# Zeros by GpSimd and twelve idle products at the start of a relative-attention and binary-FFN kernel

## The chip, the cores and the metric

The kernel runs on one core of a Trainium2 chip. The metric is the device time of one execution in microseconds (us), as the median of several runs. The core has five engines with a queue each: TensorE (PE), which multiplies matrices, VectorE (DVE), ScalarE (ACT), GpSimd (POOL) and SyncE (SP), which here only issues transfers. Engines wait for one another through semaphores.

## The reference

The input x has 16 blocks (the batch) of 512 rows with 128 features. Each row is normalised, and the result xn goes two ways. Both results are added to x.

```python
xn = _layernorm(x)
# attention: 16 heads of 8, with relative positions
xa = layernorm(xn) * ln_g + ln_b
q, k, v = xa @ Wq + bq, xa @ Wk + bk, xa @ Wv + bv
p = pe @ Wp                                    # pe: sines and cosines of the position
score = (q + u_bias) k^T + relative_shift((q + v_bias) p^T)
attn = softmax(score * 8 ** -0.5) v
out_a = attn @ Wo + bo
# FFN with weights of +1 and -1 from boolean kernels k0, k1, k2
h = relu(s0 * [xn, -xn] @ k0) * 2
h = relu(s1 * h @ k1) * 2
out = x + out_a + s2 * h @ k2
```

## The kernel before

The program has two stages. The first, up to about 240 us, normalises the blocks, runs the FFN and the projections, and writes q + u, q + v, k, p and v to DRAM in the layout that the second stage reads. The second, from there to the end, is the attention, head by head, in an order written out by hand (`STEPS`), with a few last pieces of the FFN beside its first steps.

In the first stage no order is written by hand on any engine, but for a few single edges (`issue_after`). The program is traced in the order of the source, and a planner of the framework then sets the order on each engine: of the instructions that it reckons to be ready, by its own costs of the operations and transfers, it takes the one that stands earliest in the source. The engines run their queues strictly in the order that results. An instruction that the planner reckoned ready too early so holds up all that stands behind it on its engine.

What bears on the change, in the order of the source:

- L266 to L270: `root` and `rows` are filled by VectorE, and ScalarE takes a first square root.
- L280: `qu_t` are the two tiles for the halves of q + u: `k_flat[0]`, a tile of the second stage, and `qu_l`, each of 128 x 2050 float16, zeroed as 1025 words. q + u is written to every second place in part of them, and the zeros beside it are written out with it. `after` (L274) are two places in the buffer `e_1`, in which p lies between zeros for a while. `v_t` (two tiles) are filled with ones. `q_banks` (L236) are two PSUM banks for q.
- L288 to L293: these fills. VectorE fills `qu_t` and `after`, GpSimd fills `v_t`.
- L294 to L323: SyncE issues the loads, one after the other: block 0 of x, k0, the three scales `s_cols`, k1, block 1 of x, k2, the weights, and so on.
- L325 to L330: GpSimd makes the identity `ident` and tables from it.
- L339 to L386, `norm(0)`: VectorE takes the statistics of block 0 (L365, L366), ScalarE the root (L375), VectorE the reciprocal and one refinement step (L376 to L382), then normalises the four chunks (L351). `norm(1)` and later ones are called from a queue further down, and take the statistics of blocks 1 and 2, 3 and 4 and so on.
- L395 to L407: from `s_cols` and k0 VectorE makes the factors `w_mul` and the first FFN weights (L402); ScalarE makes the second weights from k1 (L404), four instructions.
- L441 and L449: the tile `ab` of 128 x 2 x 128 float32 is filled with ones by GpSimd. One half of it is later scaled (L461), and both are the stationary operands of three products (L467 to L475), which bound the sizes of q and k.
- L530 to L541, `transposed2`: TensorE transposes the four chunks of a block (L534), ScalarE and VectorE split the result into a high and a low float16 half (L624, L625). The low half is what the high one leaves of the value.
- L659 to L662, `ffn_layer`: for each f of four, TensorE multiplies the weights with the high and then the low half (L644), and ScalarE and VectorE split the result (L621, L622).
- L485 to L499: the scales of q, k and p come out of VectorE (L487 scales Wp), and L499 is the first product of the projections.
- L664 and L694: `ffn_residual` loads x again for the sum at the end of a block, `ffn_out` adds to it (L700) and stores it (L703).

Of the kernel before, what the change touches and what calls it, by code (L numbers as in the profile page):

```python
# [9 lines left out]
F32 = mybir.dt.float32  # L10
# [9 lines left out]
B, S, D, H, DH = 16, 512, 128, 16, 8  # L20
P = 128
# [67 lines left out]
def rel_attention_and_binary_ffn(  # L89
# [38 lines left out]
    nc = tc.nc  # L128
# [102 lines left out]
    with ExitStack() as pre:  # L231
# [4 lines left out]
        q_banks = psp.tile([P, 2, S], F32, tag="q", name="q_banks")  # L236
# [8 lines left out]
        def sts(name, shape, dt=F32):  # L245
            return setup.tile(shape, dt, tag=name, name=name)
# [38 lines left out]
        qu_rows = [t[:, : 4 * S].rearrange("p (v x) -> p v x", v=2) for t in qu_t]  # L285
        v_b = [t.rearrange("p (h c w) -> p h c w", h=H, c=NC) for t in v_t]

        for t in qu_t:  # L288
            nc.vector.memset(t.bitcast(F32), 0.0)
        for t in after:  # L290
            nc.vector.memset(t.rearrange("p x u b -> p (x u b)").bitcast(F32)[:, : PAD + S // 2], 0.0)
        for t in v_t:
# [145 lines left out]
                nc.vector.tensor_copy(cols, pt[:, :10])  # L438


        ab = sts("ab", [P, 2, D])  # L441
        t_abs = sts("t_abs", [P, 3])
        w_abs = sts("w_abs", [P, 3, D])
        rows_abs = sts("rows_abs", [4, 2, P])
# [1 line left out]
        pw = sts("pw", [P, 2])  # L446
        q_mul, k_mul = pw[:, 0:1], pw[:, 1:2]
        b_cols = sts("b_cols", [P, 3])
        nc.gpsimd.memset(ab, 1.0)  # L449

        def absolute():
            for dst, src in (
# [758 lines left out]
```

## Time and profile before

| | |
|---|---|
| median of 3 runs | 1342.36 us |
| lowest, highest run | 1341.71, 1346.67 us |
| profiled execution | 1341.79 us |
| its span, first to last instruction | 1339.8 us |
| mean granted clock of TensorE | 0.994 |
| first record of TensorE | 9.86 us |
| first product of the FFN | 12.29 us |
| end of GpSimd's first fills and the identity | 2.55 us |

The profile is of one execution. Its times run from the first instruction; the execution takes 2.0 us more than its span. A group of instructions is named by its line in the source. "Busy" is the share of time in which an engine runs an instruction; records of TensorE overlap, so that for a row of products the distance from start to start says more than the length of one. A float32 product stands as two records. "The chain" is followed back from the last instruction, at each step to what released it.

### The profile page before, as it was taken

What the parts mean: (1) busy time and instruction counts of PE and PEld (TensorE: products, weight loads), DVE (VectorE), ACT (ScalarE), POOL (GpSimd) and SP (SyncE); (2) the same over time, 40 slices, a digit from 0 to 9 for tenths busy, and PEclk for the clock granted to TensorE, in tenths of its full rate; (3) what the DMA queues carried; (4) which work ended last, traced back from release to release, by engine and by line L of the source; (5) the groups of instructions that cost most, each with busy time, mean ns of one, the idle gap of its engine ahead of it and who ended that gap; (6) DMA issues with size and microseconds to landing.
All of it is one profiled execution on the core that took longest, in us unless ns stands there. A gap on an engine that the chain in (4) does not pass through costs nothing.

```text
span 1339.8 us, 55726 instructions
## 1 busy us (share of the span) xinstructions
PE 1290.1 (96%) x23065; PEld 948.2 (71%) x23065; DVE 1117.1 (83%) x2734; ACT 851.2 (64%) x1389; POOL 305.8 (23%) x520
## 2 busy tenths in 40 slices
PE   6899999889999999999999999999999999999995
PEld 3455555677777777777777777777777777777763
DVE  8999766778888888888888888888888888888874
ACT  4555666556666666666666666666666666666660
POOL 3011000112222222222233322222222222233100
PEclk9999999999999999999999999999999999999998
DMA  5576548944444444444444444444444445544443
GB/s 143 200 252 214 209 176 309 304 108 108 111 109 105 105 105 107 107 105 106 109 110 112 106 110 113 107 119 116 119 116 123 110 116 134 119 106 115 102 94 79
DMA packets 278409, 178.07 MB, mean 133 GB/s; under 512 B 113142, under 2 KB 266780, under 8 KB 278084
## 3 DMA queue, kind: packets, MB, share of 16 engines
q1 hardware_dynamic: 258940, 157.10, 42.5%
q0 software_dynamic: 16880, 16.30, 5.3%
q8 instruction: 181, 2.97, 1.0%
q10 hardware_dynamic: 2336, 1.12, 0.3%
q14 instruction: 72, 0.59, 0.2%
HBM read 113.97 MB, written 56.78 MB: 127 GB/s over the span
## 4 chain that ended last, share of the span: by engine, by line
PE 82%; DVE 8%; DMA 5%; ACT 2%; issue 1%; SPq 1%; POOL 0%; POOLq 0%; DVEq 0%; ACTq 0%
PE a_t L908 18%; PE s L881 17%; PE s L819 17%; PE s L835 12%; PE p L644 6%; PE t_t L872 4%; PE s L848 4%; DMA q<-qv_scr 1%; DVE m L867 1%; PE a_t L686 1%; DVE h2l L622 1%; DVE qu_l L526 1%; DVE xn L351 1%; PE p L579 1%; DMA rden_scr<-den 1%
## 5 line engine op out<-in xcount | busy, mean ns | idle before, releaser
L891 ACT ACTIVATE e<-s,e_scale 128x512 f32<-128x512 f32 x1024 | 672.6, 685 | 334.7 <-PE s L881 334.4
L862 DVE TENSOR_REDUCE m<-s 128x256 bf16<-128x512 f32 x512 | 351.4, 686 | 127.5 <-PE s L848 127.4
L867 DVE TENSOR_TENSOR m<-s,m 128x256 bf16<-128x256 f32 x1024 | 429.6, 420 | 18.3 <-PE s L848 0.6
L819 PE MATMUL s<-q,k 128*128 128x64 f16 x8192 | 407.0, 193 | 2.4 <-DVE e L622 1.6
L881 PE MATMUL s<-ident_b,nm 128*128 128x256 bf16 x2048 | 352.6, 274 | 2.3 <-DVE nm L876 2.3
L835 PE MATMUL s<-q,win 128*128 128x128 f16 (+1 forms) x4096 | 342.5, 206 | 0.0
L819 PEld LDWEIGHTS <-k 128*128 128x128 f16 x8192 | 335.2, 98 | 9.3 <-issue 3.0
L908 PE MATMUL a_t<-e,v 128*9 128x256 f32 x4032 | 265.3, 380 | 0.7 <-issue 0.7
L835 PEld LDWEIGHTS <-win 128*128 128x128 f16 x4096 | 232.0, 98 | 0.0
L881 PEld LDWEIGHTS <-nm 128*128 128x128 bf16 x2048 | 144.8, 98 | 118.1 <-DVE m L867 78.0
L848 PE MATMUL s<-q,win_d 128*128 128x64 f16 x2048 | 227.7, 193 | 0.0
L876 DVE TENSOR_REDUCE nm<-t_t 128x2 bf16<-128x256 bf16 x512 | 209.3, 409 | 0.6 <-PE t_t L872 0.6
L872 PE MATMUL t_t<-ident_b,m 128*128 128x128 bf16 x1024 | 141.1, 219 | 5.4 <-DVE m L867 5.3
L966 POOL DMA_DIRECT2D rden_scr<-den x58 | 32.4, 559 | 489.9 <-DVE nm L876 465.5
L908 PEld LDWEIGHTS a_t<-e,v 128*9 128x9 f32 x4032 | 86.3, 90 | 80.9 <-issue 1.5
L848 PEld LDWEIGHTS <-win_d 128*128 128x128 f16 x2048 | 129.9, 98 | 0.0
L958 POOL DMA_DIRECT2D sum_scr<-av x232 | 117.5, 513 | 0.0
L872 PEld LDWEIGHTS <-m 128*128 128x128 bf16 x1024 | 79.6, 97 | 41.3 <-DVE m L867 10.7
L644 PEld LDWEIGHTS <-e 128*128 128x128 f16 x512 | 49.5, 98 | 59.5 <-issue 11.3
L644 PE MATMUL p<-h1l,e 128*128 128x512 f16 x240 | 63.2, 381 | 0.0
L644 PE MATMUL p<-h1h,e 128*128 128x512 f16 x240 | 62.2, 379 | 0.5 <-DVE h1l L622 0.5
L622 DVE SCALAR_TENSOR_TENSOR h2l<-p,h2h 128x512 f16<-128x512 f32 x60 | 41.1, 686 | 25.9 <-ACT h2h L621 25.7
(165 smaller groups left out, 894.7 us busy)
## 6 DMA issues: line engine op xcount, KB each, us to landing
q<-qv_scr SPq DMA_DIRECT2D x512, 64.0 KB
q<-qu_scr SPq DMA_DIRECT2D x256, 64.0 KB
k<-k_scr SPq DMA_DIRECT2D x128, 128.0 KB
win<-p_scr SPq DMA_DIRECT2D x128, 79.5 KB
v<-v_scr SPq DMA_DIRECT2D x32, 288.0 KB
k_scr<-hv SPq DMA_DIRECT2D x64, 128.0 KB
qu_scr<-k SPq DMA_DIRECT2D x16, 512.0 KB
qu_scr<-qu_l SPq DMA_DIRECT2D x16, 512.0 KB
```

Source lines behind the costliest of these rows:

```text
L644: nc.tensor.matmul(ph, lhsT=w[:, t, f * P : (f + 1) * P], rhs=h[t][m], start=(m == 0 and t == 0), stop=(m == 1 and t == n - 1),)
L819: nc.tensor.matmul(sp[:, c % 2, :, :, 4 * g : 4 * g + 4].rearrange("p a r (n m) -> p n (a r) m", m=2), lhsT=kt[:, g, c * P : (c + 1) * P], ...
L835: nc.tensor.matmul(blocks[:, x0 : x0 + (NC + 1) * (len(cs) - 1) + 1 : NC + 1], lhsT=win[side_m][:, side, y0 : y0 + P], rhs=qp[:, side, :, ...
L848: nc.tensor.matmul(blocks[:, x0 : x0 + NC + 2 : NC + 1, 2 * t : 2 * t + 2], lhsT=win_d[side_m][:, t, UP_OFF - 4 * u : WIND - 4 * u], rhs=q ...
L862: nc.vector.tensor_reduce(st["max"], flat(st["ps"][0]).rearrange("p c x -> p x c"), AX.X, ALU.max)
L867: nc.vector.tensor_tensor(st["max"], flat(st["ps"][1])[:, c], st["max"], ALU.max)
L872: nc.tensor.transpose(st["pt"][:, f, :], st["max"][:, f * P : (f + 1) * P], ident_b)
L876: nc.vector.tensor_reduce(st["nm"], st["pt"], AX.X, ALU.max, negate=True)
L881: nc.tensor.matmul(flat(st["ps"][half])[:, :, f * P : (f + 1) * P], lhsT=st["nm"][:, f : f + 1].to_broadcast([P, P]), rhs=ident_b.unsqueez ...
L891: nc.scalar.activation(st["eT"][:, :, cs, :, i0 : i0 + 4].rearrange("p b c a r -> p (c a) b r"), st["ps"][half].rearrange("p c a r b -> p ...
L908: nc.tensor.matmul(bank[32 * r : 32 * r + VW, g], lhsT=v_t[pair["m"]][:, v0 : v0 + VW], rhs=pair["eT"][:, b, c], start=(c == 0), stop=(c = ...
L958: queue.dma_start(sum_scr[h, :, b : b + 2, :], av[32 * r : 32 * r + DH])
```

## The change

Three edits, all at the start of the first stage. The tile `ab` is made, and filled with ones by GpSimd, ahead of all other fills. Right behind it in the source stand twelve float32 products of `ab` with itself, 128 x 128 times 128 x 256, into the two banks of q in turn; nobody reads the results. And the zeros in `qu_t` are written by GpSimd instead of VectorE; those in `after` stay with VectorE.

```diff
+        ab = sts("ab", [P, 2, D])
+        nc.gpsimd.memset(ab, 1.0)
+        for n in range(12):
+            nc.tensor.matmul(
+                q_banks[:, n % 2, : 2 * D],
+                lhsT=ab[:, 0],
+                rhs=ab.rearrange("p n d -> p (n d)"),
+                start=True,
+                stop=True,
+            )
+
         for t in qu_t:
-            nc.vector.memset(t.bitcast(F32), 0.0)
+            nc.gpsimd.memset(t.bitcast(F32), 0.0)
         for t in after:
             nc.vector.memset(t.rearrange("p x u b -> p (x u b)").bitcast(F32)[:, : PAD + S // 2], 0.0)
...
-        ab = sts("ab", [P, 2, D])
         t_abs = sts("t_abs", [P, 3])
...
-        nc.gpsimd.memset(ab, 1.0)
```

## The prediction

> **What bounds the kernel now.** I first asked where the whole span goes, then only about the stretch that the change touches. From the page, busy time and the chain of waits:
>
> ```profile
> span 1339.8 us, 55726 instructions
> ...
> PE 1290.1 (96%) x23065; PEld 948.2 (71%) x23065; DVE 1117.1 (83%) x2734; ACT 851.2 (64%) x1389; POOL 305.8 (23%) x520
> ...
> PE 82%; DVE 8%; DMA 5%; ACT 2%; issue 1%; SPq 1%; POOL 0%; POOLq 0%; DVEq 0%; ACTq 0%
> ```
>
> TensorE carries 82% of the chain and GpSimd none. All that the change edits happens before the first product of data, so the second view is the chain in its first 17 us: start, length, what.
>
> ```profile
> 3.25 4.13 DMA xn<-in_L_attn_x_dram
> ...
> 7.41 0.29 DVE bn L365
> 7.71 0.10 DVE root L376
> ...
> 8.11 2.93 ACT e L404 x4
> 11.04 0.52 ACT e L413
> 11.55 0.12 ACT w_abs L459
> 11.67 0.58 ACT sums L624
> 12.25 0.04 issue
> 12.29 1.45 PE p L644 x3
> 13.75 0.02 issue
> 13.77 0.61 ACT h1h L621
> 14.38 0.02 issue
> 14.40 0.69 DVE h1l L622
> ...
> 16.71 5.34 PE p L644 x24
> ```
>
> No memset is in it. What ends last is the load of the second block of rows (x1): VectorE's queue has x1's statistics (L365) ahead of the reciprocal of block 0 and of the factors w_mul (L398 to L400), so both stand until 7.41. ScalarE then spends 2.93 us on the weights (L404) before it splits block 0 at 11.67. TensorE enters with three products in 1.45 us.
>
> The third view is the timeline of TensorE: the first products, later ones of the same shape, and then the half-microsecond windows (length, busy, granted clock, DMA share, GB/s).
>
> ```profile
> 12.29 1.44 PE L644 MATMUL p<-sums,w_sb 128*128 128x512 f16 x3 [0.38 <-ACT sums L624]
> ```
> ```profile
> 17.57 1.03 PE L644 MATMUL p<-h1l,e 128*128 128x512 f16 x4
> 18.43 1.03 PE L644 MATMUL p<-h1h,e 128*128 128x512 f16 x4
> ```
> ```profile
> 36.00:36.50 0.50, 0.41 (x2) 1.00 1.15 345
> ...
> 39.50:40.00 0.50, 0.00 (x0) 1.00 0.00 0
> 40.00:40.50 0.50, 0.34 (x1) 0.62 0.00 0
> ...
> 43.00:43.50 0.50, 0.50 (x3) 0.50 0.00 0
> 43.50:44.00 0.50, 0.50 (x4) 0.96 0.45 169
> ```
>
> From 17.57 to 18.43 four products start in 0.86 us, 0.215 each. The first ones start 0.43 apart, half that pace, although the clock column says 1.00 there: before the first recorded change it is no witness, the pitch is. The windows show the same gate at work: TensorE idles from 36.41 to 40.16, the clock halves at about 40.1 (3.7 us into the idle time), and comes back at about 43.5 after 3.3 us of work. The first products came to full pace somewhere between 16.2 and 16.71, some 4 us after 12.29. So the change aims at something real; the question is what hangs on it.
>
> **The change part by part.**
>
> *Zeros moved (L289).* Two VectorE memsets of 0.91 us leave, and its last early memset, which ends at 4.12, would end at 2.29. Block 0 had landed by 4.05, where its statistics start without a wait; the bytes of its load and of k0 are through by about 3.5, so its statistics gain at most 0.6 us. Then s_cols holds VectorE until 5.33 (0.27 us idle) and x1 until 7.41 (0.96 us idle). With the queue in its present order those two loads end when they did, and the 1.83 us are worth nothing.
>
> On GpSimd the same 1025 words cost about 1.03 us each, by its rows for 576 words (0.577 us) and 512 words (0.524 us): 2.05 us. Its early work ends at 2.55 and it next has to do something at 8.44, where it waits 5.9 us for Wp; the identity is first read at 8.79 (L326), and the zeros are first needed at 57 us, by the halves of q + u. So 2.05 us hide in 5.9; without that cover they would be paid in full ahead of the identity.
>
> *The ones moved up (L449).* Same instruction, 0.315 us; it ends near 1.1 us if it is first behind GpSimd's start at 0.74, and near 4.2 if the zeros and v's ones stand ahead of it (0.74 + 0.32 + 2.05 + 1.1).
>
> *Twelve products.* A float32 product of 128x256 is two records (L467: x2). No row has them alone; the float32 512-column pair of L569 takes 0.86 us at full pace, so half the columns cost 0.215 per record, or 0.43 at half pace. There are 24 records. With full pace after 3.3 to 4 us, 8 to 10 of them are slow: 1.1 + 8 x 0.43 + 16 x 0.215 = 8.0 us, or 8.4 with ten. They run where TensorE idles until 9.86. If none became fast they would take 10.3 us, to 11.4. I take 8.2, since two places of this trace show the recovery. No later instruction reads the banks, and project_q writes them on the same engine, at 57 us.
>
> *What full pace is worth at 12.29.* The first two of the three chain products start early anyway; the third needs the low half that VectorE ends at 12.97 (L625, 0.69 us from 12.28). It started at 13.10 and ended near 13.74; at full pace it starts at 13.0 and takes 0.38: 0.35 us earlier. From 14.40 VectorE is busy nearly without a gap until 40, and TensorE from 16.71 until 36.41, so whatever comes before is carried on, and nothing but the 0.35 is won by the other five products.
>
> *What the planner may do with a freer VectorE.* The order on the engines of this first stage is not written by hand (a memset of L601, which belongs to its end, stands at 6.39 before x1's statistics). If block 0 is ready sooner by the planner's reckoning, its reciprocal and w_mul go ahead of x1's statistics, which are then done in the 1.43 us that VectorE idles before 14.40. w_mul hangs on s_cols alone: it comes at about 6.6 instead of 7.72 to 8.07, and ScalarE's weights at 6.9 instead of 8.11. The reciprocal comes at 6.65, behind the root that ends at 6.62, instead of 7.62, so the first transpose moves from 9.86 to about 8.9 (behind the ones) and the last from 11.61 to about 10.4. ScalarE's split is then at 10.45 instead of 11.67: 1.2 us. Lower bound of this part nothing, upper bound 1.8 (all the memset time). I take 1.2, because the two steps blocked in that queue are ready before 6.7 in the trace, and what they wait for is the rank of one statistics instruction.
>
> Sum: 1.2 + 0.35 = 1.55 us, against the profiled execution's 1341.79 (its span of 1339.8 and 2.0 us around it): 1340.24. The median of the runs shown is 0.57 above that execution, so I say **1340.8**. The chain behind 17 us has no event of fixed time; its later loads (69.47, 121.74) are issued behind the work before them, so I carry all of it to the end.
>
> [...] The row: between the ones' end at 8.2 and the first product there are only transposes. With the old order that is 8.2 to 12.29, 4.1 us, against the 3.7 us of idleness after which the clock fell at 40.1; with the new order it is 8.2 to 11.1, 2.9 us. [...] No run here shows what transposes count for.
>
> **Rivals.**
>
> *The queue keeps its order.* For it: if x1 is reckoned as early beside block 0's root as before, nothing in the ranks changes. Only 0.35 us is won: 1341.44 against the profile, 1342.0 as a median.
>
> *The warmth is lost again.* If 3.7 us pass with transposes counted as idle, the 0.35 goes and only the rank of the statistics is left: 1341.2 as a median, or 1342.4 where that has not changed either. [...]
>
> *The ones are late.* If they start at 4.2, ten slow and fourteen fast records end at 11.5, when the rows have waited since 8.9 or 9.86; four transposes in 0.6 us end at 12.1 against 11.61. That is 0.5 us slower: 1342.9. It decides if GpSimd does the zeros first.
>
> *Slower: a hold on SyncE's queue.* Stores and loads share it, in the planner's order. Its waits show the store of the first residual (L703) held 8.3 us for VectorE's L700, to 31.84, with the next loads behind it; now that is hidden. If a moved VectorE queue ranks such a store ahead of a load that is wanted within 8.3 us, TensorE stands for it: 8.3 - 1.55 = 6.75 us slower, 1349.1. Against it: 1.8 us is little beside the leads of those loads.
>
> *Faster than forecast.* The idle 36.41 to 40.16 is a wait for VectorE's L487, whose queue is full from 14.40 on. If freed VectorE time closes that gap, 3.75 us go, and the half clock behind it (3.4 us, worth 1.7): 1.55 + 3.75 + 1.7 = 7.0, or 1335.4. Against it: TensorE's own work before the gap moves up as well, so that the gap keeps most of its length; the clock alone (1339.1) is likelier than the gap.
>
> **How the numbers follow.** Forecast 0.40, old order 0.20, warmth lost 0.08, ones late 0.08: together 0.76, all within 0.5% (6.7 us, about what a measurement of this kernel can tell from no change). The gap and its clock closed, with what follows, 0.13; the hold 0.11. The forecast's own range is 1338.5 to 1342.5. For 8 in 10 I take 1336.0, nearly all of the closed gap, to 1346.5, about the highest run of before (1346.67); that leaves out most of the hold and the end of the gap case.
>
> **What would show it.** Ones from about 1.1 us, ending before 8.5, and products at 0.215 from the first one on: the clock part. The reciprocal ahead of x1's statistics and ScalarE's L404 before 7: the queue part. L621 at 13.4 means the old order, at 12.2 the new one. A first transpose that waits for TensorE means the ones were late. I am wrong if the stretch from 285 us on starts more than 2 us off its place, or its beat differs from 4.03 us (L881 at 289.33 and 293.36 in the chain).

## The result, and the profile after

The changed kernel takes 1340.41 us (median of 20 runs, 1336.45 to 1342.89), the kernel before in the same comparison 1343.59 us (20 runs, 1339.87 to 1346.94). The ratio is 0.9975 with a 95% interval of 0.9966 to 0.9984: 3.4 us less, between 2.1 and 4.6. That is within 0.5%. A second comparison of the same two kernels (below) gave 0.9985 [0.9974, 0.9995], 2.0 us less. The profiled execution of after has a span of 1336.7 us and a time of 1338.55, against 1339.8 and 1341.79. Lines of the changed kernel stand 9 to 11 further down: L365 is L376, L404 is L415, L487 is L496, L499 is L508, L644 is L653, L668 is L677, L697 is L706.

Span, busy time and the shares of the chain of waits, after:

```profile
span 1336.7 us, 55775 instructions
...
PE 1296.0 (97%) x23089; PEld 953.5 (71%) x23089; DVE 1116.2 (84%) x2732; ACT 851.5 (64%) x1389; POOL 307.5 (23%) x522
...
PE 84%; DVE 9%; DMA 2%; ACT 2%; issue 1%; SPq 1%; POOL 0%; DVEq 0%; ACTq 0%; POOLq 0%
```

TensorE's busy time is 5.9 us longer: the 24 records of ones take 8.06 us, and all else is 2.2 us shorter. The chain at the start (start, length, what):

```profile
2.77 3.69 DMA k_r<-in_L_ffn_k_dram
...
6.55 2.40 ACT e L415 x4
...
10.90 0.49 ACT sums L633
...
11.43 1.12 PE p L653 x4
...
12.57 0.61 ACT h1h L630
...
13.20 0.69 DVE h1l L631
...
15.13 5.34 PE p L653 x24
```

The load of the second block of rows is no longer in it. ScalarE's weights start at 6.55 instead of 8.11, the split of block 0 at about 10.9 instead of 11.67, and the block of 24 products at 15.13 instead of 16.71: 1.58 us. VectorE's timeline shows why (start, length, line, operation; in brackets the idle time before it and what ended it):

```profile
4.78 0.66 DVE L412 TENSOR_TENSOR k<-k_r 128x512 f32<-128x512 uint8 x1
...
6.21 0.14 DVE L411 TENSOR_SCALAR w_mul<-sgn 128x1 f32<-128x1 f32 x1
6.27 0.19 DVE L387 RECIPROCAL root<-root 128x8 f32<-128x8 f32 x1
...
7.45 0.29 DVE L376 BATCH_NORM_STATS2 bn<-xn 128x6 f32<-128x128 f32 x1 [0.15 <-DMA xn<-in_L_attn_x_dram]
```

The factors and block 0's reciprocal now stand ahead of the statistics that wait for the second block. The subtraction of k0's halves (L412) has moved too: it now runs at 4.78, ahead of the instructions that read `s_cols`, where in before it stood behind the first of them and ahead of the factors, at 5.54. TensorE's timeline of after:

```profile
1.10 8.06 PE L291 MATMUL q_banks<-ab 128*128 128x256 f32 x24 [1.10 <-POOL ab L289]
8.99 0.71 PE L543 MATMUL p<-ident,xn 128*128 128x128 f32 x4
...
11.43 1.53 PE L653 MATMUL p<-sums,w_sb 128*128 128x512 f16 x6 [1.04 <-ACT sums L633]
```

Six products in 1.53 us: full pace from the first one on, in this execution. And the wait that I had named as the place where more could come from is there unchanged; the list of TensorE's waits (total, count, longest):

```profile
PE p L508 <- DVE wp_d L496: 3.8, 1, 3.8
```

It was 3.7 us before. The clock fell inside it again (windows: length, busy, granted clock, DMA share, GB/s), this time 2.3 us after TensorE's last product at 34.83, and stayed down until 43.96:

```profile
37.00:37.50 0.50, 0.00 (x0) 0.64 0.00 0
...
38.50:39.00 0.50, 0.37 (x1) 0.50 0.00 0
...
43.50:44.00 0.50, 0.50 (x2) 0.54 0.72 269
```

Against before, the product of wp_d starts 1.53 us earlier (38.63 for 40.16). By a beat I mean the transposes of L872 (L881 after) in one round of the attention; two rounds take 4.03 us. The first beat, at 245 us, is only 0.11 earlier, since this half clock lasted 6.8 us instead of 3.4. The twenty-fifth, near 300 us, is 1.71 earlier, since before had another fall at 272 us and after has none there. The beat itself is the same.

### The profile page after: what moved, and what is told of

It reads as the page before. It is cut to its first block, busy times and chain, and to the rows that moved or that the text cites. A ratio compares the mean times of both kernels' runs of the same rounds, so it can differ in the third digit from the quotient of the medians.

```text
span 1336.7 us, 55775 instructions
## 1 busy us (share of the span) xinstructions
PE 1296.0 (97%) x23089; PEld 953.5 (71%) x23089; DVE 1116.2 (84%) x2732; ACT 851.5 (64%) x1389; POOL 307.5 (23%) x522
## 4 chain that ended last, share of the span: by engine, by line
PE 84%; DVE 9%; DMA 2%; ACT 2%; issue 1%; SPq 1%; POOL 0%; DVEq 0%; ACTq 0%; POOLq 0%
PE a_t L917 18%; PE s L890 18%; PE s L828 17%; PE s L844 12%; PE p L653 6%; PE t_t L881 4%; PE s L857 4%; DVE m L876 1%; PE a_t L695 1%; DVE h2l L631 1%; DVE qu_l L535 1%; DMA q<-qv_scr 1%; DVE xn L362 1%; PE p L588 1%; PE q_banks L559 1%
## 5 line engine op out<-in xcount | busy, mean ns | idle before, releaser
L881 PE MATMUL t_t<-ident_b,m 128*128 128x128 bf16 x1024 | 140.9, 219 | 5.5 <-DVE m L876 5.5
L881 PEld LDWEIGHTS <-m 128*128 128x128 bf16 x1024 | 79.5, 97 | 41.2 <-DVE m L876 10.8
L653 PEld LDWEIGHTS <-e 128*128 128x128 f16 x512 | 49.4, 98 | 59.2 <-issue 10.8
L653 PE MATMUL p<-h1l,e 128*128 128x512 f16 x240 | 63.2, 381 | 0.0
L630 ACT ACTIVATE h2h<-p 128x512 f16<-128x512 f32 x60 | 35.7, 596 | 43.1 <-PE p L653 43.0
L653 PE MATMUL p<-h1h,e 128*128 128x512 f16 x240 | 62.2, 379 | 0.6 <-DVE h1l L631 0.6
```

Of the source, the lines that this page charges most:

```text
L653: nc.tensor.matmul(ph, lhsT=w[:, t, f * P : (f + 1) * P], rhs=h[t][m], start=(m == 0 and t == 0), stop=(m == 1 and t == n - 1),)
L881: nc.tensor.transpose(st["pt"][:, f, :], st["max"][:, f * P : (f + 1) * P], ident_b)
```

## The experiments

My theory after the result: the start is worth what was forecast, and the spread of the rest hangs on where the granted clock falls while TensorE idles. The rival: one half of the change does it all. In the table, the ratio is to before in the same comparison, "block" is the start of the block of 24 products, "wp_d" that of the product that waited, "wait" TensorE's wait ahead of it, all in us of one profiled execution.

| kernel | ratio to before [95%] | median us | block | wp_d | wait |
|---|---|---|---|---|---|
| before | 1 | 1343.59 | 16.71 | 40.16 | 3.7 |
| whole change | 0.9975 [0.9966, 0.9984] | 1340.41 | 15.13 | 38.63 | 3.8 |
| the same again | 0.9985 [0.9974, 0.9995] | 1341.50 | 15.92 | 39.46 | 3.8 |
| zeros only | 0.9963 [0.9949, 0.9976] | 1339.06 | 15.20 | 37.48 | 2.1 |
| zeros only, again | 0.9965 [0.9952, 0.9978] | 1338.12 | 15.41 | 37.73 | 2.2 |
| ones only | 0.9992 [0.9979, 1.0005] | 1342.31 | 16.81 | 39.73 | 2.8 |
| zeros, later fills | 0.9964 [0.9950, 0.9977] | 1338.53 | 15.39 | 37.70 | 1.6 |
| whole, less GpSimd work | 0.9943 [0.9925, 0.9960] | 1334.96 | 15.25 | 34.81 | none |

**Each half alone, the whole again, and the gap filled** (one chip; before 1343.01 us, 33 runs). Zeros only is before with

```diff
         for t in qu_t:
-            nc.vector.memset(t.bitcast(F32), 0.0)
+            nc.gpsimd.memset(t.bitcast(F32), 0.0)
```

> The zeros in qu_t by GpSimd, no products, ab where it was. Queue theory (the rank of block 0's reciprocal and of w_mul before x1's statistics is most of the gain at 17 us): L404 starts at about 6.6 instead of 8.11, first FFN product about 11.4 instead of 12.29, products still 0.43 apart, the block of 24 products at 15.5 to 15.6 instead of 16.71; the median 1.1 to 1.2 us below before. Rival, the clock is what pays: block of 24 at 16.3 or later, median no more than 0.5 us below before. Rival, the rest of the 3.2 us lies in the zeros: median 3 us below.

Measured: 0.9963, better than the whole change. TensorE's first products:

```profile
11.53 2.72 PE L644 MATMUL p<-sums,w_sb 128*128 128x512 f16 x6 [0.70 <-ACT sums L624]
...
15.20 1.21 PE L644 MATMUL p<-h1h,e 128*128 128x512 f16 x4
```

Six products in 2.72 us, half pace, and yet the block of 24 starts at 15.20: the zeros alone give 1.51 us of the 1.58. Only half of that is the earlier entry that I forecast: the first product comes at 11.53 for 12.29, 0.76 us. The other half lies behind it, from the first product to the block (3.67 us here, 4.42 in before), in VectorE's order. Its low halves (L622), first in before and then with the zeros alone:

```profile
14.40 0.69 DVE L622 SCALAR_TENSOR_TENSOR h1l<-p,h1h 128x512 f16<-128x512 f32 x1 [1.43 <-ACT h1h L621]
15.01 0.47 DVE L365 BATCH_NORM_STATS2 bn<-xn 128x6 f32<-128x128 f32 x2
...
16.00 0.66 DVE L622 SCALAR_TENSOR_TENSOR h1l<-p,h1h 128x512 f16<-128x512 f32 x1
```
```profile
13.76 0.68 DVE L622 SCALAR_TENSOR_TENSOR h1l<-p,h1h 128x512 f16<-128x512 f32 x1
...
14.52 0.63 DVE L622 SCALAR_TENSOR_TENSOR h1l<-p,h1h 128x512 f16<-128x512 f32 x1
```

In before the statistics of later blocks stand between the first two low halves; with the zeros alone they are done by then.

Ones only is before with the tile of ones, its fill and the twelve products of the change, and the zeros left on VectorE.

> The tile of ones first and the twelve products, the zeros still by VectorE. Queue theory: reciprocal still behind x1's statistics at 7.4, L404 at 8.1, products 0.215 apart from the first one on, block of 24 products at 16.3 to 16.4 (0.35 us won); the median 0.3 to 0.5 us below before. Rival, the clock pays (also in later stretches, because an early start moves the points at which the gate decides): median 2 to 3 us below before.

Measured: 0.9992, no difference. The products of ones ended at 7.95; the windows then show

```profile
10.50:11.00 0.50, 0.44 (x2) 0.81 1.04 323
11.00:11.50 0.50, 0.50 (x2) 0.50 1.05 313
```

The clock had fallen at 10.8, behind 1.9 us of idleness and some transposes, before the first product at 12.31; the products started 0.43 apart as without the ones. The warmth was lost.

> The changed kernel once more, to see what of its profile recurs. All theories: the block of 24 products at 15.13. Theory that the points at which the clock falls and rises lie anywhere against the kernel: the fall beside the wait for L496 comes at another time than 37.15 and the rise at another than 43.9, and the time won between 40 and 300 us differs from the first profile's by 1 to 2 us. Rival, the points are fixed by when TensorE starts: fall and rise again within 0.3 us of 37.15 and 43.9. The step of 1.3 us near 1146 us (before waits there, the changed kernel does not): back if it is tied to the program's instructions, gone if it is chance.

Measured: 0.9985. In this execution the same kernel lost its warmth: the ones ended at 8.24, TensorE was busy with transposes for 1.7 us between 8.48 and 10.55, and the clock fell at 11.39, just ahead of the first product:

```profile
11.46 2.72 PE L653 MATMUL p<-sums,w_sb 128*128 128x512 f16 x6 [0.91 <-ACT sums L633]
...
15.92 1.02 PE L653 MATMUL p<-h1h,e 128*128 128x512 f16 x4 [0.58 <-DVE h1l L631]
```

The block comes at 15.92, 0.8 us behind the warm execution, though the first product starts at the same time (11.46 for 11.43). So in the order that the changed kernel has, full pace is worth 0.8 us; but that order is the slower one, since at half pace the zeros alone are 0.7 us ahead of it. The ones are a bet: won, the block comes at 15.13 to 15.25 (three executions), about where the five executions of kernels with the zeros and without the ones have it (15.17 to 15.41); lost, at 15.92 and 16.04.

The clock's fall beside the wait came at 38.69 and its rise at 45.52, not at 37.13 and 43.96, so these points are not fixed by the program. The step near 1146 us came back (0.75 us at 1146.15, before 0.68 at 1145.82), so the change does not remove it.

The fourth put eight unread float32 products into the gap, ahead of the wait for wp_d, so that the clock should not fall there:

```diff
+        def between():
+            with tc.issue_after(last_bound[0].ins):
+                for n in range(8):
+                    nc.tensor.matmul(
+                        q_banks[:, n % 2, : 2 * D],
...
             lambda: transposed2(2),
+            between,
             positions,
```

> The changed kernel with eight more unread products of ones into the banks of q, ahead of the last products that TensorE has before it waits for L496 (wp_d). Theory that the half clock at 37 to 44 us costs: no fall of the clock there, the pair of L499's float32 products in 1.1 us or less instead of 2.05, and from 45 us on 1.5 to 3 us ahead of the changed kernel; the median 1.5 to 2.5 us below the changed kernel's, 4.5 to 6 below before. Rival, VectorE bounds that stretch and full pace only waits for it a little later: the pair fast, but less than 0.7 us ahead at 100 us and no measurable difference from the changed kernel.

Measured: 0.9988 [0.9975, 1.0001], 1340.57 us. The products stand where they should and the product of wp_d starts at 38.63 as in after, at full pace; but the wait only moves behind it, to 40.5:

```profile
PE p L666 <- DVE h2l L644: 5.7, 6, 2.9
```

The clock then fell at 43.9. The order changed as well: wp_d was ready at 35.2, and the unread products and eight others stood ahead of its product. TensorE was not the one in want of time here: it stood 2.9 us for VectorE, and unread products fill a hole without closing it.

**The rank alone, the zeros again, and GpSimd quiet** (one chip; before 1343.82 us, 28 runs). The fifth keeps every fill on VectorE and only puts the statistics of the second block behind the factors and block 0's refinement:

```diff
-                    nc.vector.bn_stats(bn, xn_all[b][:, c, :])
+                    with tc.issue_after(first["w"].ins) if (b, c) == (1, 0) else nullcontext():
+                        with tc.issue_after(first["step"].ins) if (b, c) == (1, 0) else nullcontext():
+                            nc.vector.bn_stats(bn, xn_all[b][:, c, :])
```

> The kernel before with one edge more: VectorE's first statistics of x1 stand behind w_mul (L403 here) and block 0's refinement step (L382). Zeros stay with VectorE, no products. Theory that this rank is what the moved zeros win at the start: L404's successor here (the weights on ScalarE) starts at 6.7 to 6.9 instead of 8.11, the block of 24 products at 15.2 to 15.6 instead of 16.71, as with the zeros alone (15.20). Rival, the memset time itself is worth something: block of 24 not before 16. For the whole: if the start is carried, 1.2 to 1.5 us below before; if the length of the wait for wp_d decides (3.7 us before, 2.1 with the zeros alone), no more than that although the zeros alone gave 5.

Measured: 0.9994 [0.9980, 1.0007]. The block came at 16.26: 0.45 us of the 1.51, all of it by the first product (11.85). The factors were ready at 7.4 only, as VectorE's rows show:

```profile
5.89 0.17 DVE L398 TENSOR_SCALAR sgn<-s_cols 128x2 f32<-128x2 f32 x1 [0.83 <-DMA s_cols<-in_L_ffn_s_dram]
...
6.10 0.69 DVE L404 TENSOR_TENSOR k<-k_r 128x512 f32<-128x512 uint8 x1
```

VectorE idles 0.83 us for `s_cols` with all its fills in place, so the fills' time is not what keeps the factors; the subtraction (L404) is, which here still stands behind `s_cols` and ahead of them. With the zeros moved the planner changed that rank too, and the rank of the second low half. So the one rank that I had named is a part of the gain, and the rest is other ranks.

> The zeros alone, once more. Theory that their order of VectorE's queue shortens the wait for wp_d: L499 again at 37.3 to 37.7, TensorE idle 2.0 to 2.3 us before it, whatever the phase of the clock; median 3 to 5 us below before, that is 1 to 3 below the changed kernel's. Rival, the first result was luck of the clock: no more than 2 us below before.

Measured: 0.9965. That the zeros alone beat the whole change stands: the two pairs average 0.9964 against 0.9980, with some 0.0012 of uncertainty on the difference.

Why does VectorE's queue reach wp_d so late? Two timelines of after, VectorE's and GpSimd's, in the stretch ahead of the wait:

```profile
27.89 2.20 DVE L706 TENSOR_SCALAR once<-once,f_c 128x4 f32<-128x4 f32 x1
29.08 1.11 DVE L709 SCALAR_TENSOR_TENSOR sums<-a_t,once,sums 128x128 f32<-128x128 f32 x4
30.12 1.21 DVE L383 TENSOR_SCALAR var<-st 128x8 f32<-128x8 f32 x1
...
31.31 0.22 DVE L706 TENSOR_SCALAR once<-once,f_c 128x4 f32<-128x4 f32 x1
...
35.50 2.06 DVE L490 TENSOR_SCALAR bmax<-bmax 128x2 int32<-128x2 int32 x1
36.56 1.01 DVE L392 TENSOR_TENSOR step<-var,root 128x8 f32<-128x8 f32 x1
```
```profile
27.88 1.26 POOL L677 TENSOR_TENSOR sums<-sums,bo_sb 128x512 f32<-128x512 f32 x1
29.08 0.98 POOL L526 MEMSET q<- 128x512 f32 x2
30.03 1.27 POOL L677 TENSOR_TENSOR e<-e,bo_sb 128x512 f32<-128x512 f32 x1
...
35.36 1.26 POOL L677 TENSOR_TENSOR sums<-sums,bo_sb 128x512 f32<-128x512 f32 x1 [4.06 <-DMA sums<-in_L_attn_x_dram]
36.56 0.99 POOL L526 MEMSET q<- 128x512 f32 x2
```

In before VectorE has the same rows:

```profile
29.47 2.20 DVE L697 TENSOR_SCALAR once<-once,f_c 128x4 f32<-128x4 f32 x1
30.66 1.11 DVE L700 SCALAR_TENSOR_TENSOR sums<-a_t,once,sums 128x128 f32<-128x128 f32 x4
31.70 1.20 DVE L372 TENSOR_SCALAR var<-st 128x8 f32<-128x8 f32 x1
...
37.13 1.26 DVE L381 TENSOR_TENSOR step<-var,root 128x8 f32<-128x8 f32 x1
```

The same operation of VectorE, four words to a partition, takes 2.20 us at 27.89 and 0.22 at 31.31. The record of the long one ends at 30.09, with GpSimd's pair of fills, the next ends with GpSimd's addition at 31.30, and the one at 35.50 with the pair at 37.55. VectorE stands there, and the profile counts it as busy. It does not stand for the whole length of a record: the four instructions behind the first one (L709) start from 29.08 on, when GpSimd's addition ends, at their usual distance of 0.26 us. Counted from the start of a held instruction to the start of the next one, less the usual distance, an addition cost up to 1.1 us, and a pair of fills between nothing and 0.9. In after and in before that makes some 3.9 us ahead of wp_d, in the two executions of the zeros alone some 2.4. This fits their wait, which is 1.6 us shorter; it isn't shown to be its only cause, since the ones alone stood 3.8 us with a wait of 2.8. For the additions the trace shows it on one operation (L706): 1.19 us to the next start beside one, at 27.89, and 0.13 without, at 31.31. Operations of other kinds kept their length beside three additions from 23.27 to 26.99 (L631 0.68 us, L376 0.26).

So the seventh, on top of the whole change, takes this work of GpSimd's out of the stretch; it leaves out the additions of seven blocks, so that it also does less work:

```diff
-            last = nc.gpsimd.tensor_tensor(
+            if 6 <= b < LAST:
+                last = nc.gpsimd.tensor_tensor(
...
-            if 2 <= b < 10:
+            if 6 <= b < 14:
```

> The changed kernel without GpSimd's additions of bo for blocks 0 to 5 and 15 (left out of the output there), and with the zeros of the q tiles (L517) moved behind block 6, so that GpSimd does nothing between 20 and 45 us. Theory that GpSimd holds VectorE (L706 in 2.2, L383 in 1.2, L490 in 2.06 us, each ending with a GpSimd instruction): those three in 0.16 to 0.25 us, no VectorE instruction over 0.75 us between 20 and 40, L508 (the product behind wp_d) at 34 to 36 instead of 38.63, TensorE idle before it less than 1 us; 3 to 5 us ahead of the changed kernel at 45 us. Rival, those three wait for something else (a result of ScalarE or TensorE): they stay over 1 us and L508 stays within 0.7 us of 38.6.

Measured: 0.9943, 7.7 us less than before. VectorE's timeline now has

```profile
28.01 0.20 DVE L707 TENSOR_SCALAR once<-once,f_c 128x4 f32<-128x4 f32 x1
...
33.48 0.16 DVE L490 TENSOR_SCALAR bmax<-bmax 128x2 int32<-128x2 int32 x1
```

All three holds are gone (2.20 to 0.20, 1.21 to 0.16, 2.06 to 0.16), wp_d's product starts at 34.81 without a wait, and the beat near 300 us is 5.4 us ahead of after's.

> The zeros alone, and the zeros of the q tiles (L517) moved from behind blocks 2 to 9 to behind blocks 6 to 13: same work, out of the first 45 us on GpSimd. If GpSimd holds VectorE also while it fills: L499 1 to 2 us earlier than with the zeros alone (37.48), median 1 to 2 us below theirs, a version ahead of both kernels. Rival, only GpSimd's additions (which read) hold VectorE: L499 within 0.5 us of 37.5. Rival, the fills hold VectorE later on instead: L499 earlier, but the same median.

Measured: 0.9964, the same as the zeros alone, and L499 at 37.70, as the rival had it in which only additions hold VectorE. The fills by themselves are not it: the additions still held VectorE's L697 for 1.2 us and its L480 for 0.9.

**The additions on VectorE** (one chip; before 1342.08 us, 11 runs). The ninth takes the late fills and the zeros, and gives the additions of those blocks to VectorE:

```diff
-            last = nc.gpsimd.tensor_tensor(
+            eng = nc.gpsimd if 6 <= b < LAST else nc.vector
+            last = eng.tensor_tensor(
                 rows_of, rows_of, bo_sb.unsqueeze(1).to_broadcast([P, NC, D]), ALU.add
             )
-            if 2 <= b < 10:
+            if 6 <= b < 14:
```

> Before with the zeros beside q + u and p on GpSimd, the fills of the query tiles moved from behind blocks 2 to 9 to behind blocks 6 to 13, and the addition of bo for blocks 0 to 5 and the last one issued on VectorE instead of GpSimd; no ones. All of the output is computed. Theory (GpSimd's long operations hold VectorE): the quiet variant was 5.4 us ahead of the changed kernel at the beat of 24 because its VectorE was not held; here six additions come to VectorE's queue, some 1.0 to 1.3 us each, of which four or five lie ahead of the product of wp_d, and none is held 2.1 us beside GpSimd. So that product comes at 36 to 38 us, the wait ahead of it is 0 to 2 us, and the ratio lies between the zeros alone and the quiet variant: 0.994 to 0.9965. Rival (it is only the amount of work, wherever it is done): the product at 38.5 us or later and a ratio of 0.9965 or more.

Measured: 0.9937 [0.9924, 0.9950], 1334.51 us. Its page and two of its VectorE rows:

```profile
span 1334.4 us, 55721 instructions
...
PE 1290.0 (97%) x23065; PEld 949.9 (71%) x23065; DVE 1114.5 (84%) x2739; ACT 852.1 (64%) x1389; POOL 299.4 (22%) x515
```
```profile
29.48 0.66 DVE L669 TENSOR_TENSOR sums<-sums,bo_sb 128x512 f32<-128x512 f32 x1
...
33.73 0.22 DVE L698 TENSOR_SCALAR once<-once,f_c 128x4 f32<-128x4 f32 x1
```

An addition takes VectorE 0.66 us and GpSimd 1.26. Against before, VectorE has seven additions more (4.6 us) and two fills less (1.8 us), and yet is busy 2.6 us less (1114.5 for 1117.1): by this sum some 5.4 us of what stood there as busy was standing. The product of wp_d starts at 34.62 without a wait, earlier than the 36 to 38 that I expected, and the ratio is just below the expected 0.994 to 0.9965.

> The quiet variant without the twelve products of ones and with the ones tile where it was before: zeros on GpSimd, fills of the query tiles behind blocks 6 to 13, the addition of bo left out for blocks 0 to 5 and the last one (their bias is missing in the output). Theory: with VectorE no longer held there is no wait ahead of wp_d in either, so the ones decide only the pace and the order of the first products: the block of 24 at 15.2 to 15.4 as in the quiet variant (15.25), the product of wp_d at 34.8 to 35.5, and a ratio within 0.001 of the quiet variant's 0.9943. Rival (the ones cost something by themselves, since zeros alone were better than the whole change): a ratio of 0.993 or less. Rival (the ones win something once the wait is gone): 0.9955 or more.

Measured: 0.9959 [0.9947, 0.9972], 1337.51 us, the product of wp_d at 35.83. By its number this is the rival "the ones win something once the wait is gone"; but the two intervals (0.9947 to 0.9972 and 0.9925 to 0.9960) overlap, and this kernel does less work than the ninth and came out behind it. I take it as inconclusive.

**What the change is worth where nothing holds VectorE ahead of 45 us** (one chip; before 1342.87 us, 11 runs). The whole change, and nothing of it, each with the edit of the ninth.

> The whole change (zeros on GpSimd, twelve products of ones), with the query tiles' fills behind blocks 6 to 13 and the addition of bo for blocks 0 to 5 and the last one on VectorE. Against the same without the ones (0.9937, 1334.51 us) this prices the ones alone where nothing holds VectorE. Theory (the ones cost and win little by themselves; their loss in the whole change was the wait ahead of wp_d): the product of wp_d within 1 us of 34.8, no wait of over 1 us ahead of it, and a ratio of 0.9925 to 0.9945. Rival (the ones' order costs about 1.5 us by itself): 0.995 or more. Rival (the full pace at the first products, about 1 us, shows once the wait is gone): 0.993 or less.

Measured: 0.9942 [0.9926, 0.9958], 1334.63 us, as the theory had it, though the product of wp_d came at 36.38, 1.6 us off the 34.8, with no wait of its own. The warmth was lost once more (ones until 8.38, first product at 11.60, block at 16.04):

```profile
11.50:12.00 0.50, 0.40 (x2) 0.66 1.03 305
12.00:12.50 0.50, 0.50 (x3) 0.50 0.25 68
```

> The kernel before with nothing of the change: its zeros on VectorE, no products of ones; only the query tiles' fills behind blocks 6 to 13 and the addition of bo for blocks 0 to 5 and the last one on VectorE. It prices the zeros' move where nothing holds VectorE. Theory (the start's 1.5 us is carried on as it is): the block of 24 at 16.7 instead of 15.2, the product of wp_d at 36.3, and a ratio about 0.0011 above the 0.9937 with the zeros moved: 0.994 to 0.996. Rival (the freed stretch to 40 us takes the start's gain up): the same ratio, 0.993 to 0.994. Rival (the hold matters little by itself and only together with the zeros): 0.9975 or more.

Measured: 0.9935 [0.9923, 0.9948], 1334.69 us: the number of the first rival, not of the theory. With the block at 16.73 and wp_d's product at 39.37 (no wait) the profiled execution is 4.4 us behind the ninth's at the first beat, 2.8 at the twenty-fifth (the ninth's clock had fallen near 274 us) and 1.0 at the end; the medians of both agree. With, without, and with half of the change the three medians are 1334.51, 1334.63 and 1334.69 us. On each difference the intervals leave some 0.002, 2.5 us, so the start's 1.5 us may be there; it doesn't show. Where the start's lead goes between the first beat and the end in that kernel stays open. With GpSimd's additions in place the zeros alone had won 4.8 us (0.9964 in two comparisons); here they win nothing, with 2.5 us to either side. So most of what they won went through the holds, or through the order of the queues around them; no run separates the two. The same is open for the 8.7 us that this kernel wins by the moved additions and fills: here, as in the ninth and the eleventh, VectorE has 20 statistics of chunks ahead of wp_d, in before 25, so the order changed along with the holds.

## Why the prediction was right or wrong

The number (1340.8 us for 1340.41 measured, and 1341.50 in the repeat) and its class, no difference over 0.5%, came out, the number in part by luck: I had started from a median of 1342.36 for before, which was 1343.59 over 20 runs, and the change won 3.4 us, or 2.0 in the repeat, where I had added up 1.55. The sum behind it came out in part.

- **The queue part** was the right mechanism: reciprocal and factors ahead of the second block's statistics, ScalarE's weights at 6.55 (I had 6.9). Its size in the zeros alone is 1.51 us, where I took 1.2, but it is made up otherwise: the first product came 0.76 us earlier, and 0.75 us more was won behind it, for which my sum has no term. What failed is the step "what they wait for is the rank of one statistics instruction": that rank alone won 0.45, and the subtraction and the second low half changed their ranks as well. That the fills' time by itself is worth nothing, no run contradicts.
- **The clock part** was mis-sized: 0.35 forecast. In the order of the changed kernel full pace was worth 0.8 (15.13 for 15.92), but against the zeros alone, which have another order, the ones stand 0.07 ahead with the warmth and 0.7 behind without it. I had compared the pace of three products in an order that the change does not keep.
- **The warmth is lost again** had a chance of 0.08, and was tied to 3.7 us of idleness. Of six profiled executions with the ones, three lost it (ones only, the repeat, the eleventh) and three kept it, two of those being the gap filled and GpSimd quiet. What tells them apart is the time from the ones' end to the first product: 2.3 to 2.5 us where it was kept (after 9.16 to 11.43, the gap filled 9.11 to 11.52, GpSimd quiet 9.03 to 11.56), 3.2 to 4.4 us where it was lost (the repeat 8.24 to 11.46, the eleventh 8.38 to 11.60, ones only 7.95 to 12.31). The row that I had missed is in the trace of before: its clock steps at 40.12, 43.53, 272.23 and 275.65 lie multiples of 3.413 us apart, to within 0.05 us (the two falls are 232.11 us apart, 68 times that), and so do those of the repeat, at 11.39, 14.80, 38.69, 45.52 and 274.21, and the two of after, at 37.13 and 43.96. The repeat's fall beside the wait came 1.56 us later than after's, in the same kernel. So 3.7 us was the idleness ahead of one fall, not a measure for the next: in after the clock fell 2.3 us behind TensorE's last product, and in the first run of the zeros alone it read 1.00 from 30 to 45 us, with a wait of 2.1 us in that stretch. What a transpose counts for isn't shown; the repeat's clock fell with 1.7 us of transposes between the ones and the fall.
- **The ones** ended at 9.16 in the profiled execution, past my 8.0 to 8.4: by their pitch (0.43 us a record until then, 0.215 from there) the clock rose at 6.4, 5.3 us after they began, where I had reckoned with 3.3 to 4. They took 8.06 us there, and between 6.85 and 8.01 in the five others. The first normalised chunk of after was ready at 8.33 and waited 0.66 us for TensorE, to 8.99. That lay beside ScalarE's own work, which ran until the split at 10.81, and cost nothing.
- **The ones late, the queue keeping its order, the hold on SyncE's queue**: none of them came. GpSimd made the ones first, at 0.74 to 1.05, and its zeros ended at 2.83.
- **The gap and its clock.** I had written that the gap would keep its length, since TensorE's work moves up as well. For the whole change that held (3.8 for 3.7 us), for the zeros alone not (2.1), and that is where they beat the whole change: their product of wp_d starts 1.15 us ahead of after's. The wrong step was the sentence "from 14.40 VectorE is busy nearly without a gap until 40". It was recorded as busy; by the rows of before at 29.47, 31.70 and 37.13, shown above, and the distances to the next starts, it was standing for some 3.9 us. I read busy time as work.
- **The sum.** It was −1.55, the two comparisons gave −3.4 and −2.0. What makes the whole change's mean larger than its start is not settled: single executions of one kernel differ by several us. The two profiled executions of the changed kernel took 1338.55 and 1343.92 us, at a mean granted clock of 0.993 and 0.99, and the second had two falls of the clock more, near 11 and 274 us. Twenty runs average over that.

## What to carry to other kernels

Before counting an engine's busy time as work, compare the lengths of one and the same small operation along the timeline; where a 0.2 us row takes 2 us, look at what the engine beside it is doing at that time, and count the stall up to the start of the next instruction. Here the edit that removed those stalls (seven short additions moved from GpSimd to VectorE, and sixteen fills put later) was worth 8.7 us (0.9935) with nothing of the change in it, more than twice the change. The unread products bought full pace in the three executions in which the first real product came within 2.5 us of their end, and not in the three in which it came 3.2 us behind it or later; price such products by the loss as well as by the win, in several executions.

## What the runs showed of the hardware that I had not expected

- VectorE operations of 0.16 to 0.22 us lasted 1.2 to 2.2 us beside GpSimd's additions (1.26 us) and fills (0.5 us each), and were back to 0.16 to 0.20 us with GpSimd idle. The next instruction started up to 1.1 us late for an addition; the record of a held one can run on to the end of the fills behind it, though VectorE works again (L709 from 29.08 on).
- VectorE's splits (0.68 us) and statistics (0.26 us) kept their length beside the same additions.
- The steps of the granted clock within one execution lay multiples of 3.41 us apart (before: 40.12, 43.53, 272.23, 275.65); the fall in after came 2.3 us into TensorE's idle time, the one in before 3.7.
- The clock column reads 1.00 until the first recorded step, while the products' pitch of 0.43 us shows half pace (zeros alone, 11.53 to 14.25).
